# Strassen block products for layer 0's values, a ring of PSUM banks, and new hand-written orders in a two-layer attention kernel

## The chip, the cores and the metric

The kernel runs on one core of a Trainium2 chip. The metric is the device time of one launch in microseconds; lower is better. All large products are in float32. The engines are PE (TensorE matmul; its weight loads are listed as PEld), DVE (VectorE), ACT (ScalarE), POOL (GpSimd) and SP (SyncE, which here only issues DMAs).

## The reference, cut to what matters

```python
# layer 0: x is (8, 512, 32, 32): 8 batches, 512 channels, 1024 tokens
h = group_norm(x, 32 groups)                       # (8, 512, 1024)
q, k, v = einsum('oc,bcn->bon', qkv_w, h) + qkv_b  # 8 heads of 64
attn = softmax(q^T k / 8)                          # 1024 x 1024 per head
x = x + einsum('oc,bcn->bon', proj_w, attn v) + proj_b
# layer 1
importance = sum over channels of x*x;  idx = the 256 tokens of highest importance
q_sel, k_sel = layer_norm(wq x[idx]), layer_norm(wk x[idx]);  v = wv x
attended = softmax(clip(q_sel k_sel^T / sqrt(512))) v[idx]
x = x + wo (v with the columns idx replaced by attended)
```

## The kernel before

**Layer 0.** The unit of work is one pair of heads and one half (512) of the queries: 8 batches x 4 pairs x 2 halves = 64 units. In a unit, PE makes the scores of 8 blocks of 128 keys against 512 queries of two heads (`scores`), ACT copies them out of PSUM, DVE keeps the running maximum and subtracts it, ACT takes the exponential, POOL adds up the denominators (`add`), and PE multiplies with the values (`values`). Between these, PE does side work that other units need. `side(t)` lists up to seven pieces for unit t, and each has a `fill` (its matmuls) and an `empty` (one copy or add out of PSUM). They are

- q and k of a later pair, by `query_key`: Strassen's scheme with seven block products, four emptied by ACT and three by an add on DVE. It multiplies token sums (`combine_tokens`, made by POOL once per batch) with weight sums (`combine_weights`, made once at the start, stored in DRAM and loaded again tile by tile with `load_weights`, two ahead, on SP's queue);
- v for two pairs, a tile `vs[m]` of 1024 tokens x 256 columns, by `v_tokens`: four parts of two token blocks each, one per unit, all by plain products. A part is 16 calls of matmul with 64 token columns as weights and 256 columns streamed; float32 makes two instructions of each call;
- the output projection of the batch before, by `project_out`, in four of the eight units of a batch.

All side work goes through one PSUM bank (`ps_g`, one buffer); the chain of block products 1, 6, 7, 4 and that of 5, 3 stay in the bank from one fill to the next. The score tiles in SBUF, tagged "e", have 14 buffers (`ep`).

The order of everything in a unit is written out in the string `SLOT`: a word is a step, and each `+` or `-` says that it is done for a unit later or earlier. Each engine executes its instructions in this order.

**Layer 1** is ordered in the same way by the strings `BATCH` (one pass per batch) and `END` (the last two batches). The steps that are named later: `row` (four transposes of 128 tokens by PE) with `square` and `keep` (ACT) and `put` (DMA); `xs` (token sums by POOL); `va` to `vf` (PE: v by seven block products, `va` holds two of them) and `ka` to `kg` (ACT copies and DVE adds that take them); `count`, `place` and `pick` (DVE: rank of each token, and the 0/1 matrices that pick the highest 256); `holder` and `who` (indices of the picked tokens); `getx` and `getv` (gathers by POOL); `qk`, `stats`, `root`, `norm`, `normt`, `scale`, `score`, `clip`, `exp`, `probt`, `att`, `attk`, `attput` (the attention among the picked tokens); `fetch` (POOL puts the results in place), `back` (four transposes by PE) and `add` (DVE adds the residual and the result is stored). Every PE step of layer 1 writes one of eight PSUM banks, taken in `bank` from the pool "g" with eight buffers; which free bank is taken is left to the framework.

The tile for each v product of layer 0 is reached through these lines of `side`:

```python
m, part = divmod(t, 2 * NH)
...
if t and m + 1 < PAIRS // 2:
    todo[4] = v_tokens(m + 1, part)
```

Of the kernel before, what the change touches and what calls it, by code (L numbers as in the profile page):

```python
# [10 lines left out]
F32 = mybir.dt.float32  # L11
# [3 lines left out]
ALU = mybir.AluOpType  # L15
AX = mybir.AxisListType
PSUM = bass.MemoryType.PSUM
DRAM = bass.MemoryType.DRAM

P = 128  # L20
# [31 lines left out]
keep5+ val5- empty5- mix2- val4- sub1 sub6 fill0 empty0 den- take- mix1-- sc7+ out- exp6 var-  # L52
exp1 fac-- mean- sub0 sc6+ max6+ mix4- fill1 exp0 sub7 empty1 val6 max7+ val1 fill2 add1 add6
inv- app0- keep6+ exp7 keep7+ sub3 sub2 empty2 sc3+ app1- exp3 exp2 sc4+ fill3 mix3 max3+ stat1-
val7 empty3 add7 div- max4+ keep3+ keep4+ val0 fill4 add2 empty4 sc0++ turn+ neg+ sub5 sc1++
keep0++ add3 fill6 keep1++ val3 sub4 val2 exp5 add5 empty6 sc5++ max1++ sc2++ exp4 stat2+ add4
fill5 stat0 keep2++ spread0+ max5++ max2++
# [7 lines left out]
vput6- put4 keep2 back6--- row3 square3 square1 xs0 keep3 put3 keep1 put1 inv-- back7--- xs1 va1  # L65
back4--- row5 va0 add3--- ka0 add4--- att0-- vb0 kb0 ka1 row0 vput4- attk0-- row7 add6--- vd0
square0 holder- keep0 vc0 att1-- vb1 add7--- row6 who- kc0 put0 kg0 square7 kb1 kf1 keep7
square6 ve0 vd1 attk1-- va2 kd0 getx- vc1 square5 finite keep5 spread0 vput0- kc1 xs2 attput--
vput2- spread1 put2 vf1 ka2 vb2 kg1 kf0 vput3- imp0 imp1 fetch1-- count4 va3 count6 selt0-
selk0- fetch5-- selt1- fetch4-- ve1 vput7- selk1- keep6 count0 ka3 ke1 kf3 count1 kd1 qk1-  # L70
stats1- fetch0-- xs3 put5 qk0- count7 root1- fetch3-- qk2- norm1- kb2 put7 qk3- stats0- stats2-
root0- norm0- fetch2-- vd2 root2- kf2 back2-- stats3- fetch6-- norm2- kc2 fetch7-- vc3 vf0 vb3
root3- vput1- add2-- normt0- norm3- back5-- kb3 count2 vf2 back0-- ke0 vput5- ke2 normt1- add5--
normt2- vd3 scale2- vc2 normt3- scale0- add0-- scale3- kc3 put6 back1-- add1-- scale1- count3
kg3 score0- score1- row4+ square4+ keep4+ vf3 kg2 row1+ ve3 clip- kd3 ve2 kd2 count5 getv-
back3-- row2+ exp0- probt- ke3 square2+ place pick0 probk- pick1
"""
END = """
keep2- inv--- row5- row7- put4- put2- row0- row6- square1- keep1- att1--- holder-- square7-
who-- put1- attk1--- keep7- att0--- row3- put7- attk0--- square5- square6- square0- square3-  # L80
finite- va3- row0 attput--- keep5- keep3- back4---- getx-- xs2- spread0- add3---- vput0-- keep0-
xs3- add4---- back7---- back6---- fetch4--- put0- add7---- add6---- spread1- selt0-- imp0- imp1-
row7 selk0-- count3- selt1-- selk1-- qk0-- ka3- row4 put3- count6- qk1-- keep6- count0- square0
fetch0--- fetch5--- vput1-- stats0-- qk2-- keep0 root0-- row1 row6 count4- stats1-- norm0--
square7 put5- keep7 put6- put0 stats2-- root1-- count1- fetch3--- square1 root2-- square4 row5
va2- keep1 kf3- vput6-- square5 norm1-- ka2- put1 vput3-- keep4 vb3- qk3-- norm2-- fetch1---
count2- keep5 normt0-- put7 square6 kf2- fetch7--- row2 vput2-- count7- stats3-- kb3- vb2- put4
vc2- scale0-- keep6 row3 vd3- square3 kb2- vput7-- put6 va0- count5- square2 root3-- vd2- vc3-
kc2- finite fetch6--- keep3 kg2- vf2- ke2- keep2 spread0 fetch2--- place- norm3-- vput5-- ve2-
normt1-- vput4-- scale1-- kc3- spread1 kd2- xs0- va1- ka0- back2--- imp0 normt3-- pick1- pick0-  # L90
vput6- imp1 holder- kg3- scale3-- normt2-- vf3- scale2-- score1-- who- score0-- vb0- ka1- getx-
put5 ve3- kf0- count3 add2--- back6--- kb0- getv-- count5 clip-- vd0- kd3- vc0- selt0- put3 kc0-
xs1- add6--- count2 exp0-- back3--- kg0- vb1- probt-- selk0- selt1- vf0- count6 probk-- ke0-
selk1- put2 qk2- back7--- add3--- count1 ve0- kf1- ke3- count0 kb1- att1-- inv-- count7 attk1--
add7--- att0-- count4 back1--- place qk1- pick0 pick1 attk0-- kd0- qk0- holder who vd1- vc1-
back0--- kc1- getx stats0- stats1- attput-- fetch1-- fetch5-- root1- add0--- fetch4-- add1---
va2 vf1- root0- qk3- kg1- vput4- norm0- xs2 norm1- selt1 selt0 selk0 normt0- ve1- stats3- selk1
qk1 kd1- fetch2-- root3- fetch0-- stats1 normt1- ke1- norm3- vput7- scale1- stats2- back5--- qk3
qk2 root2- add5--- norm2- scale0- stats3 normt3- vput2- fetch3-- normt2- vput0- back0-- scale3-
scale2- vput1- vput3- root3 root1 back4--- qk0 score0- stats2 score1- vput5- ka2 kf2 norm1 root2  # L100
add0-- stats0 add4--- root0 back4-- xs3 norm3 va3 norm2 vb2 clip- vsel1 getv- fetch6-- norm0
back6-- add6-- exp0- normt2 normt3 kb2 ka3 normt1 add4-- vd2 probt- vb3 inv- probk- normt0
scale0 att0- scale2 att1- scale1 kb3 scale3 attk1- attk0- vc2 kc2 fetch7-- kg2 back5-- attput-
vf2 fetch7- ke2 score1 score0 fetch0- va0 vselk1 fetch2- ve2 back3-- ka0 clip exp0 back2-- vsel0
add5-- probt vd3 fetch6- inv vselk0 xs0 back1-- kc3 probk kf3 vc3 att0 add2-- add1-- att1 add3--
fetch3- fetch1- attk0 va1 attk1 kg3 back4- ve3 ka1 attput fetch5- back7-- kd2 kf1 fetch4- kd3
vb0 back6- kb0 kf0 vc0 add6- xs1 vb1 vd0 kb1 add7-- vd1 kc0 vf0 kc1 kg0 fetch6 ke0 vc1 ve0 kg1
ve1 fetch3 fetch2 add4- back3- fetch4 kd0 vf1 kd1 back2- fetch0 add3- add2- back5- ke1 vf3
back1- back0- fetch1 back7- add0- back0 add7- back4 back6 add5- add1- ke3 add0 fetch5 back2
fetch7 add4 add6 back7 back5 add2 add7 add5 back3 back1 add1 add3  # L110
# [3 lines left out]
def in_order(text):  # L114

    steps = []
    for word in text.split():
        name = word.rstrip("+-")
        ahead = word.count("+") - word.count("-")
        kind = name.rstrip("0123456789")  # L120
        steps.append((kind, ahead, int(name[len(kind):] or 0)))
    return steps


@with_exitstack
def attention_then_topk_attention(
# [103 lines left out]
    def bank(key):  # L230
        if key not in tiles:
            tiles[key] = pools["g"].tile(
                [P, C], F32, tag="g", name="b_" + "_".join(map(str, key))
            )
        return tiles[key]

# [19 lines left out]
    def keep_row(b, j):  # L256
        nc.scalar.copy(tiles["xT", b, j], tiles["pt", b, j])

# [19 lines left out]
    def imp(b, j):  # L278
        t = get("rp", ("imp", b), [P, N], "imp", 1)
        nc.scalar.copy(t[:, ts(j, HALF)], tiles["pi", b, j])  # L280

# [42 lines left out]

    def vkeep(b, j):
        nc.scalar.copy(values_of(b)[:, j, :], tiles["pv", b, j])

    SPAN = C // 2  # L330
# [1156 lines left out]
```

## Time and profile before

| what | value |
|---|---|
| median of 3 runs | 2411.2 us (2409.63 to 2411.27) |
| profiled execution | 2408.76 us, span of its instructions 2407.1 us |
| granted TensorE clock | 0.994 |
| busy share of the span | PE 98%, PEld 42%, DVE 80%, ACT 59%, POOL 60% |
| groups with most PE time | scores (L1133) 513.0 us, values (L1208) 488.4 us, q and k (L926) 231.0 + 169.8 us, v of layer 0 (L845, 128x256) 217.4 us, output projection (L845, 128x512) 208.2 us |

The durations come from the profiled execution. Its matmuls are pipelined: the mean of one matmul is its own latency, and the busy time of a group is the time in which at least one of it was in flight. "128*64 128x256" means weights of 128 rows and 64 columns, and an output of 128 partitions x 256 elements. Idle time stands before the instruction that ended it, with what released it.

### The profile page before, as it was taken

How to read it: one execution, taken by the hardware profiler on the slowest of the kernel's cores; microseconds unless marked ns; L12 is line 12 of the kernel's file. 1: busy time of each engine (PE TensorE's matmuls, PEld its weight loads, DVE VectorE, ACT ScalarE, POOL GpSimd, SP SyncE). 2: the span in 40 equal slices, each digit the busy share in tenths (PEclk: the TensorE clock that was granted, in tenths of full speed). 3: DMA queues.
4: the chain of work that ended last, by engine and by line, in shares of the span. 5: the costliest groups of instructions: out<-in, count | busy, mean ns of one | idle time of the engine just before them, and what ended most of it. 6: DMA issues, size and time to landing. Idle time of an engine off the chain costs nothing. (4 is left out here: it accounts for less than half of the span.)

```text
span 2407.1 us, 33474 instructions
## 1 busy us (share of the span) xinstructions
PE 2348.3 (98%) x11820; PEld 1012.5 (42%) x11820; DVE 1917.2 (80%) x3054; ACT 1429.8 (59%) x1948; POOL 1433.8 (60%) x885
## 2 busy tenths in 40 slices
PE   6999999999999999999999999999999989999998
PEld 2333333333333333333333333333333357777766
DVE  4989987897889779887988898788777467777885
ACT  2677766676577557756766676567666434333521
POOL 1568765875677567656766676577656434444343
PEclk9999999999999999999999999999999999999999
DMA  4122122212221222222212312212223434666654
GB/s 175 36 54 78 51 69 77 87 54 71 78 84 52 73 73 89 61 69 84 74 59 72 101 48 63 76 60 82 77 65 119 166 133 149 201 205 203 237 163 153
DMA packets 184391, 235.82 MB, mean 98 GB/s; under 512 B 40970, under 2 KB 94986, under 8 KB 184224
## 3 DMA queue, kind: packets, MB, share of 16 engines
q1 hardware_dynamic: 158560, 190.12, 24.5%
q10 hardware_dynamic: 18144, 31.48, 3.5%
q0 software_dynamic: 7520, 12.09, 1.9%
q8 instruction: 93, 1.52, 0.3%
q14 instruction: 74, 0.61, 0.1%
HBM read 174.08 MB, written 72.09 MB: 102 GB/s over the span
## 5 line engine op out<-in xcount | busy, mean ns | idle before, releaser
L1200 POOL TENSOR_TENSOR es<-es,e 128x1024 f32<-128x1024 f32 x384 | 918.5, 2392 | 133.0 <-ACT e L1195 112.8
L1141 ACT COPY e<-sc 128x1024 f32<-128x1024 f32 x512 | 508.1, 1013 | 241.0 <-PE sc L1133 158.2
L1192 DVE TENSOR_TENSOR e<-e,ns 128x1024 f32<-128x1024 f32 x512 | 600.2, 1205 | 6.4 <-ACT ns L1188 6.3
L1147 DVE TENSOR_TENSOR high<-sc,high 128x1024 f32<-128x1024 f32 x384 | 467.8, 1218 | 119.3 <-PE sc L1133 79.0
L1195 ACT ACTIVATE e<-e 128x1024 f32<-128x1024 f32 x512 | 520.5, 1060 | 26.1 <-DVE e L1192 18.3
L1133 PE MATMUL sc<-q,k 64*128 64x512 f32 x2048 | 513.0, 617 | 3.1 <-DVE high L1147 1.8
L1208 PE MATMUL av<-e,v 128*64 128x512 f32 x2048 | 488.4, 597 | 0.3 <-ACT e L1195 0.3
L1200 POOL TENSOR_TENSOR es<-e,e 128x1024 f32<-128x1024 f32 x64 | 152.5, 2383 | 487.6 <-PE g L926 316.9
L1133 PEld LDWEIGHTS sc<-q,k 64*128 64x128 f32 x2048 | 174.0, 185 | 285.6 <-issue 162.3
L1208 PEld LDWEIGHTS av<-e,v 128*64 128x64 f32 x2048 | 137.5, 136 | 310.1 <-issue 274.6
L926 PE MATMUL g<-wqkv,mix 128*64 128x512 f32 x960 | 231.0, 602 | 1.7 <-POOL wqkv L890 1.2
L845 PE MATMUL g<-wqkv,x 128*64 128x256 f32 x1920 | 217.4, 379 | 0.0
L845 PE MATMUL g<-o,wp 128*64 128x512 f32 x912 | 208.2, 598 | 0.0
L845 PEld LDWEIGHTS g<-wqkv,x 128*64 128x64 f32 x1920 | 137.8, 137 | 95.1 <-issue 27.8
L926 PE MATMUL g<-x,mix 128*64 128x512 f32 x720 | 169.8, 592 | 0.0
L977 DVE SCALAR_TENSOR_TENSOR xr<-g,pb,xr 128x512 f32<-128x512 f32 x56 | 42.1, 752 | 108.5 <-PE g L845 108.5
L926 PEld LDWEIGHTS g<-wqkv,mix 128*64 128x64 f32 x960 | 60.8, 136 | 156.0 <-issue 104.7
L385 ACT COPY V<-b_px 128x256 f32<-128x256 f32 x112 | 40.0, 376 | 141.5 <-PE b_px L371 104.7
L845 PEld LDWEIGHTS g<-o,wp 128*64 128x64 f32 x912 | 60.5, 136 | 140.7 <-issue 119.2
L472 PE MATMUL b_pp<-w,selT 128*128 128x512 f32 x256 | 112.3, 593 | 0.0
L1147 DVE TENSOR_TENSOR high<-sc,e 128x1024 f32<-128x1024 f32 x64 | 77.8, 1215 | 39.9 <-ACT e L1141 39.9
L964 ACT COPY v<-g 128x512 f32<-128x512 f32 x60 | 35.1, 585 | 123.2 <-PE g L845 123.1
(217 smaller groups left out, 2628.1 us busy)
## 6 DMA issues: line engine op xcount, KB each, us to landing
nb<-negd SPq DMA_DIRECT2D x128, 256.0 KB
x<-in_x_dram SPq DMA_DIRECT2D x32, 512.0 KB
ri<-rid SPq DMA_DIRECT2D x128, 128.0 KB
sx<-xT ACTq DMA_DIRECT2D x64, 256.0 KB
mix<-mixd SPq DMA_DIRECT2D x120, 128.0 KB
xr<-in_x_dram SPq DMA_DIRECT2D x58, 256.0 KB
x1d<-xr SPq DMA_DIRECT2D x58, 256.0 KB
sv<-V ACTq DMA_DIRECT2D x56, 256.0 KB
```

The costliest lines, as they stand in the source:

```text
L385: nc.scalar.copy(out_, bank(("px", b, i))[:, :SPAN])
L472: nc.tensor.matmul(pp, tiles["selT", b][:, k, ts(rb, P)], w["qk"[which]][:, k, :], start=(k == 0), stop=(k == CT - 1),)
L845: nc.tensor.matmul(out[r, :], wide_[:, r], moving, start=(k == 0), stop=(k == CT - 1),)
L926: nc.tensor.matmul(pt[r, :], weights[:, k, r], moving[:, k, :], start=(first and k == 0), stop=(k == 1), skip_group_check=True,)
L977: nc.vector.scalar_tensor_tensor(xr, po, pb[:, mt : mt + 1], xr, ALU.add, ALU.add,)
L1133: nc.tensor.matmul(sc[:, hh, :], ks[p][r, ts(j, P)], qs[p][r, ts(hf, HALF)], start=True, stop=True,)
L1141: nc.scalar.copy(raw[t, j], banks["s", t, j])
L1147: nc.vector.tensor_tensor(high[t], banks["s", t, j], raw[t, 0] if j == 1 else high[t], ALU.max)
L1192: nc.vector.tensor_tensor(raw[t, j], raw[t, j], high[t], ALU.add)
L1195: nc.scalar.activation(raw[t, j], raw[t, j], AF.Exp, scale=QK_SCALE)
L1200: nc.gpsimd.tensor_add(sums[t], raw[t, 0] if j == 1 else sums[t], raw[t, j])
L1208: nc.tensor.matmul(avs[t][HD * hh : HD * hh + HD, :], vs[p // 2][:, j, (p % 2) * P + HD * hh : (p % 2) * P + HD * hh + HD], e[:, hh, :], s ...
```

## The change

It has four parts.

1. v of the tiles m = 2 to 15 (all of batches 1 to 7) is made by `value_product0`: seven block products, with the token sums that q and k use already. A product is again 16 calls of matmul with 64 token columns as weights, but streams 128 columns. Four of the seven are copied out by ACT, three are added by DVE. The weight sums for v are made and stored by `combine_weights` beside those for q and k, and products 6, 7, 5 and 3 load theirs with `load_weights`; 1, 2 and 4 read `wqkv`. `v_tokens` stays for the tiles 0 and 1.
2. `products_of(t)` spreads the side work anew: of the eight units of a batch, the first gets four products of v, the second one, the third two, the seventh four, the eighth three. q and k stay where they were, and so does the output projection.
3. A class `Ring` hands out the eight banks of layer 1 and the 14 score tiles of layer 0: it gives the buffer that was given back first in the order of the program, by explicit `done` and `give` calls.
4. `SLOT`, `BATCH` and `END` are new orders of the same steps.

```diff
+class Ring:
+    def __init__(self, pool, tag, shape, n):
+        self.pool, self.tag, self.shape = pool, tag, shape
+        self.free, self.held = collections.deque(range(n)), {}
+    def take(self, key, name, uses=1):
+        i = self.free.popleft()
+        self.held[key] = [i, uses]
+        return self.pool.tile(self.shape, F32, tag=f"{self.tag}{i}", name=name, bufs=1)
+    def give(self, key):
+        if key in self.held:
+            self.held[key][1] -= 1
+            if not self.held[key][1]:
+                self.free.append(self.held.pop(key)[0])
...
+            pools["banks"] = Ring(ps, "bank", [P, C], 8)
...
+            scored = Ring(ep, "e", [P, 2, HALF], 14)
...
+            def products_of(t):
+                p, hf = divmod(t, NH)
+                b, at = divmod(t, NPAIR * NH)
+                plan = [None] * 7
+                if t and hf == 0 and p + 1 < PAIRS:
+                    plan[:3] = [("qk", p + 1, i) for i in ROUND[4:]]
+                elif hf == 1 and p + 2 < PAIRS:
+                    plan[:4] = [("qk", p + 2, i) for i in ROUND[:4]]
+                later = [n for n in FILLS if n > 2]
+                if at in (0, 6):
+                    m, places, which = 2 * b + 1 + at // 6, later, ROUND[:4]
+                elif at == 1:
+                    m, places, which = 2 * b + 1, [4], ROUND[4:5]
+                elif at == 2:
+                    m, places, which = 2 * b + 1, [3, 4], ROUND[5:]
+                elif at == 7:
+                    m, places, which = 2 * b + 2, [n for n in later if n > 3], ROUND[4:]
+                else:
+                    return plan
+                if 2 <= m < PAIRS // 2:
+                    for n, i in zip(places, which):
+                        plan[n] = ("v", m, i)
+                return plan
...
+            def value_product0(m, i):
...
+                def fill(pt):
+                    tokens = tokens_of(b, i)
+                    if i in MIXED:
+                        weights = mixed.pop(("v", m, i))
+                        load_weights()
+                    else:
+                        k, which = INPUT_WEIGHTS[i]
+                        weights = wqkv[:, 2 * k : 2 * k + 2, ts(2 * CT + 2 * hm + which, P)]
+                    for j in range(NB // 2):
+                        for k in range(2):
+                            for r in range(2):
+                                nc.tensor.matmul(
+                                    pt[ts(r, HD), ts(j, P)],
+                                    tokens[:, k, j * P + r * HD : j * P + r * HD + HD],
+                                    weights[:, k, :], start=(first and j + k == 0), stop=(k == 1),
+                                    skip_group_check=True,
+                                )
+                def empty(pt):
...
+                    if i in (1, 6, 7, 4):
+                        nc.scalar.copy(out, pv)
+                    else:
+                        nc.vector.tensor_tensor(out, pv, out, ALU.add)
```

The new `SLOT` takes PE's steps in this order: val5-, fill0, den-, sc7+, sc6+, fill1, val1, val0, fill2, sc3+, sc4+, fill3, val6, val2, fill4, sc0++, sc1++, val7, fill6, val3, sc5++, sc2++, fill5, val4. Before it was val5-, val4-, fill0, den-, sc7+, sc6+, fill1, val6, val1, fill2, sc3+, sc4+, fill3, val7, val0, fill4, sc0++, sc1++, fill6, val3, val2, sc5++, sc2++, fill5.

The end of `BATCH` and, where the next pass begins, its start; before:

```
... normt3- scale0- add0-- scale3- kc3 put6 back1-- add1-- scale1- count3 kg3 score0- score1- row4+
square4+ keep4+ vf3 kg2 row1+ ve3 clip- kd3 ve2 kd2 count5 getv- back3-- row2+ exp0- probt- ke3
square2+ place pick0 probk- pick1
vput6- put4 keep2 back6--- row3 square3 square1 xs0 keep3 put3 keep1 put1 inv-- back7--- xs1 va1
back4--- row5 va0 add3--- ka0 add4--- att0-- vb0 kb0 ka1 row0 vput4- attk0-- row7 add6--- ...
```

and after:

```
... normt3- kc3 vc3 kg2 scale2- scale3- back0-- score1- ke0 score0- row4+ add0-- put6 kg3 vf3 ve3
count3 square4+ clip- ve2 getv- kd3 keep4+ row1+ count5 place exp0- row2+ ke3 back3-- kd2 pick1
probt- square2+ pick0 probk-
row3 vput0- square3 put4 square1 inv-- xs0 va1 va0 keep3 back4--- put3 xs1 keep1 back7---
back6--- vput3- add3--- keep2 att0-- ka1 ka0 kf0 add4--- kf1 attk0-- row0 vb0 square0 kb0 keep0
att1-- put0 put1 vc0 add6--- vd0 kc0 holder- row6 row7 square7 add7--- row5 vb1 ...
```

## The prediction

> **What bounds the kernel now.** I read the page's totals first, then the busy times by stretch, then the groups by shape, then the timeline where the change acts.
>
> ```profile
> span 2407.1 us, 33474 instructions
> ...
> PE 2348.3 (98%) x11820; PEld 1012.5 (42%) x11820; DVE 1917.2 (80%) x3054; ACT 1429.8 (59%) x1948; POOL 1433.8 (60%) x885
> ```
>
> The stretches (us from the start; busy time and instructions of PE, PEld, DVE, ACT, POOL; granted clock, DMA share, GB/s) say where PE's idle 59 us lie:
>
> ```profile
> 240.00:1650.00 1410.00, 1410.00 (x7284) 506.82 (x7282) 1194.24 (x1560) 950.99 (x1133) 942.75 (x419) 1.00 0.23 70
> 516.00:540.80 24.80, 24.80 (x132) 8.98 (x130) 24.34 (x33) 18.41 (x22) 17.85 (x8) 1.00 0.16 49
> 540.80:574.00 33.20, 33.20 (x171) 12.04 (x170) 24.71 (x33) 20.16 (x25) 17.81 (x8) 1.00 0.23 72
> 638.10:669.30 31.20, 31.20 (x166) 11.18 (x165) 26.45 (x33) 18.38 (x21) 24.84 (x11) 1.00 0.22 74
> 2057.00:2118.40 61.40, 58.53 (x284) 43.79 (x284) 44.37 (x130) 23.55 (x59) 26.25 (x44) 0.97 0.63 213
> ```
>
> Row 1 is the middle of layer 0: PE has work in flight throughout. Rows 2 to 4 are three of a batch's eight units (one head pair, one half of the queries); all eight take 24.8, 33.2, 31.2, 32.9, 31.2, 26.0, 24.8 and 26.0 us, and PE is busy in all of each. So layer 0 lasts as long as PE streams, and a microsecond of matmul taken out there is one off the span, as long as DVE stays below PE. It is close in row 2 (24.34 of 24.80). Row 5 is one batch of layer 1: 2.9 us of PE idle, and clock 0.97.
>
> How fast PE streams is read from unbroken runs in the timeline (start, length, operation), for today's v and, later, for transposes:
>
> ```profile
> 705.20 0.20 PEld L1208 LDWEIGHTS av<-e,v 128*64 128x64 f32 x4 [0.76 <-issue]
> 705.68 0.14 PEld L1208 LDWEIGHTS av<-e,v 128*64 128x64 f32 x2 [0.28 <-issue]
> 706.54 0.14 PEld L845 LDWEIGHTS g<-wqkv,x 128*64 128x64 f32 x2 [0.29 <-DVE high L1147]
> 706.97 3.62 PE L845 MATMUL g<-wqkv,x 128*64 128x256 f32 x32
> 2234.94 1.78 PEld L247 LDWEIGHTS b_pt<-ident,x 128*128 128x128 f32 x16
> 2235.04 1.91 PE L247 MATMUL b_pt<-ident,x 128*128 128x128 f32 x16
> ```
>
> A v part is 32 instructions, 16 pairs: two 64-column halves of the array work side by side. Less the last one's 0.38, 3.62 us are 15 steps of 0.216: 256 columns a pair. The transposes stream 128 columns, each with a load of its own: (1.91 - 0.27)/15 = 0.109 us. Half the columns take half the time.
>
> **Part 1: v by seven products.** Two v tiles per batch, batches 1 to 7: 14 tiles. Before, a tile is 4 parts x 16 pairs x 0.216 = 13.8 us. After, it is 7 products x 16 pairs, each streaming 128 columns: at 0.109 that is 12.2. Saved 1.6 us a tile, 14 x 1.6 = 22.2 us, all on the path.
>
> The trace shows no 64-wide pair at 128 columns, so its spacing is the unknown. Below: 0.107, half of 0.216 without the fixed part. Above: 0.141, if each matmul waits for its own load to end (a pair of loads shows 0.14). I take 0.109. The transposes' single loads last as long (1.78 us for 16 is 15 x 0.109 + 0.14) and yet keep 0.109, so the matmul does not wait for a load's shown end; and four loads in 0.20 us, where two take 0.14, mean that a second pair starts 0.06 after the first. Loading occupies a half for about 0.06 of 0.109.
>
> A rule speaks against this: the Trainium skill, "TensorE: Matmul & The Clock Gate", section "Back-to-back issue gap", gives streams of load and matmul about 81 ns at 128 columns against 56 ns for a matmul alone. Those 25 ns on each pair would make an estimated 0.134 x 112 = 15.0 us a tile, and the change 17 us slower in layer 0; the transposes above, at 0.109 with a load each, do not show such a surcharge.
>
> The new products need no further change of array form: each sits beside an av group, 128*64 too, and the first loads of g (706.54) go out while av still runs.
>
> **Part 2: what rides along.** ACT keeps 4 copies of 128x512 per tile (0.585 each): nothing. DVE gets 3 adds per tile, 42 x 0.69 (the q and k adds at L945) = 29 us, beside PE. Per unit, PE loses a part (3.45) and gains 4, 1, 2, 0, 0, 0, 4, 3 products of 1.745: 28.3, 31.5, 31.2, 29.5, 27.7, 22.6, 28.3, 27.8 us. DVE's fullest unit becomes the fifth, 26.45 of 27.7 (95%), where it was the first (98%); the third and eighth, with two and three adds, reach 26.3 of 31.2 and 25.2 of 27.8. So PE stays the bound. If that cover went, the adds would cost up to 29 us.
>
> 56 more weight loads of 128 KB go through SP, behind the stores and reloads of the maxima and sums, which wait for DVE and ACT. They go out two fills ahead, as q and k's do now, for which PE never idles: nothing; uncovered, the nearest row is a 0.8 us weight-load wait on a DMA, 14 x 0.8 = 11 us. At the start POOL makes four more sums, half the size of L900's 2.34 us, 4.7 us together, and SP four more stores behind them. POOL's first adds are some 60 us in, and it is busy for 10.8 of the first 60 us: nothing; uncovered, 5 us.
>
> **Part 3: layer 1, ring and orders.** The same matmuls, so only waits can change.
>
> ```profile
> PE b_pt L247 <- DVE y L625: 8.5, 3, 2.8
> ```
> ```profile
> 2113.43 1.89 PE L371 MATMUL b_px<-w,x 128*128 128x256 f32 x8
> 2114.20 3.64 DVE L407 TENSOR_SCALAR pick<-iota_f,place 128x256 bf16<-128x256 f32 x8
> ...
> 2115.16 0.60 PE L617 MATMUL b_po<-ident,V 128*128 128x128 f32 x4
> ...
> 2117.84 1.26 DVE L625 TENSOR_TENSOR y<-b_po,y 128x512 f32<-128x512 f32 x2
> 2118.56 1.12 PE L247 MATMUL b_pt<-ident,x 128*128 128x128 f32 x4 [2.80 <-DVE y L625]
> ```
>
> Three times a row transpose waits 2.8 us for its PSUM bank, which add frees; add stands on DVE behind eight picks. The granted clock then drops for a while: 0.97 over 61.4 us is 1.8 us. Together 4.6, three times: 13.9 us.
>
> What decides is the time from the last score matmul to that transpose. PE before: nine groups of four transposes (0.44), three value products (4 x 0.216 = 0.86) and one va (1.73) make 8.3 us. DVE before: clip, takes, count5, place, pick and the first add take from 2107.3 to 2118.5, 11.2 us. 11.2 - 8.3 = 2.9, which is the wait. In the new order row5 has moved back. Following take and done through it, the first row that gets an add's bank is row0, which gets add3's; it comes after nine transpose groups, the three products, two va (3.5) and att0 (1.7): 11.7 us. DVE has the same steps ahead of add3, and count3, now before clip, with add0 and kg3 takes 3.1 of the 3.45 us of the scores. So 11.2 against 11.7: the wait should go, with only 0.5 us in hand; next come the banks of add4, add6 and add7, each with two or more us in hand. I keep 1 us a boundary: 11 us saved. Bounds: 13.9 saved, and below nothing as much lost if another bank is late.
>
> The last two batches (END) are reordered too. PE idles 14 us from 2180 on; some 9 of these are waits in END that an order can gain, and as much could be lost: I take nothing.
>
> **Sum.** The profiled execution: 2408.8 us, span 2407.1. 2408.8 - 22.2 - 11 = 2375.6. It lies 2.4 under the median of 2411.2, so the forecast is 2378.
>
> **Rivals.** (a) *The weight loads set the pace.* At 0.141 a pair, a tile takes 15.8 us; against the forecast 14 x 112 x 0.032 = 50 us, so 2428, slower. It decides from 0.130 a pair, where layer 0's loss eats layer 1's 11 us. For it: no such pair is in the trace. Against it: transposes and load spacing. (b) *Ring and orders give layer 1 nothing*: the bank still waits for an add, or another wait takes its place. For it: 0.5 us in hand. Then 2389. (c) *The side bank is handed over late.* All side work shares one bank, and 50 instead of 44 fills per batch pass through it; a product's 1.7 us is half a part's. With 0.3 us exposed on each of 98 products, 29 us: 2407. Against it: two units of each batch hand over seven times already, with no idle PE.
>
> **How the numbers follow.** Forecast 0.72, (a) 0.07, (b) 0.13, (c) 0.08. Low end: 22.2, 13.9 and 9 all gained, 2366; I put 2365. High end: (b) with 9 us lost in END and a few on (c)'s way: 2402. The rest of (c) and (a) lie beyond. About 0.2% (5 us) is what a measurement of this kernel tells from no change. Faster: the forecast, (b), and a little of (c): 0.87; within: 0.03; slower: (a) and the rest of (c): 0.10.
>
> **What would show it.** v's matmuls: 16 pairs in about 1.9 us. Units of 28.3, 31.5, 31.2, 29.5, 27.7, 22.6, 28.3, 27.8 us, PE busy in all of each; layer 0 some 22 us shorter. No PE wait on add in layer 1 and no lowered clock between batches. A v group of 2.3 us or more, or PE idle before g in layer 0, would prove me wrong.

## The result, and the profile after

The kernel after takes 2419.4 us (median of 7 runs, 2413.3 to 2421.4) against 2411.3 us before: 1.0030 times the time, 95% interval 1.0019 to 1.0041. A second set of 10 runs gave 2414.2 us, ratio 1.0022 (1.0011 to 1.0032). The forecast was 2378 us. The change makes the kernel slower by 5 to 8 us instead of faster by 33.

The profiled execution of after took 2421.0 us, its span 2419.1. From the page's totals:

```profile
span 2419.1 us, 36720 instructions
...
PE 2332.1 (96%) x13164; PEld 1055.1 (44%) x13164; DVE 1970.2 (81%) x3096; ACT 1423.0 (59%) x1948; POOL 1437.9 (59%) x889
```

PE's busy time did fall, by 16 us, while the span grew by 12. So the work was saved, and PE idled 28 us more. The busy times by stretch say where. The columns are as in the prediction; the rows are the middle of layer 0, then the first, second, fourth, fifth and sixth unit of one batch:

```profile
240.00:1650.00 1410.00, 1388.85 (x8476) 545.16 (x8474) 1233.27 (x1589) 936.04 (x1123) 933.89 (x416) 1.00 0.24 75
```
```profile
526.10:554.30 28.20, 28.20 (x232) 13.95 (x230) 25.71 (x32) 19.72 (x25) 17.81 (x8) 1.00 0.18 53
554.30:585.80 31.50, 31.50 (x174) 11.55 (x173) 23.29 (x32) 19.58 (x24) 17.79 (x8) 1.00 0.25 76
617.00:646.70 29.70, 29.70 (x142) 9.29 (x140) 28.02 (x41) 19.86 (x24) 18.30 (x8) 1.00 0.27 82
646.70:675.10 28.40, 28.22 (x130) 8.67 (x128) 27.07 (x33) 17.77 (x20) 23.08 (x10) 1.00 0.25 80
675.10:701.20 26.10, 23.26 (x106) 6.88 (x104) 21.13 (x27) 19.04 (x24) 22.42 (x11) 1.00 0.41 133
```

In the middle of layer 0, PE was in flight for all of 1410 us before; now it idles 21 us. The first, second and fourth unit last what was predicted (28.3, 31.5, 29.5), and PE fills them. The fifth and the sixth were predicted at 27.7 and 22.6; over batches 1 to 6 they average 29.3 and 25.5. In the fifth, DVE is busy for 27 to 29 us; in the sixth nothing is near full, so a chain of waits sets the length. The eight units then sum to 231.3 us a batch; before they took 230.0, and 226.9 were predicted. For comparison, the fourth and the sixth unit of a batch before:

```profile
605.20:638.10 32.90, 32.90 (x172) 11.75 (x170) 26.08 (x41) 20.52 (x25) 18.69 (x8) 1.00 0.23 72
669.30:695.30 26.00, 26.00 (x139) 9.41 (x137) 20.96 (x27) 20.26 (x25) 18.34 (x10) 1.00 0.39 134
```

What PE waits for most in that stretch of after (us, times, longest); before had no entry there:

```profile
PE sc L1265 <- DVE high L1279: 10.3, 9, 1.9
PE den L1359 <- ACT e L1273: 6.1, 4, 1.8
```

The price of a product was right. In the timeline (start, length), 16 pairs of 128 columns take 1.92 us, (1.92 - 0.27)/15 = 0.110 a pair, where 0.109 was assumed:

```profile
539.34 1.92 PE L1064 MATMUL g<-mix_v,wqkv 128*64 128x128 f32 x32
```

**A DVE operation that became up to 3.5 times as long.** L805 before and L851 after are the same instruction, the group norm's apply; each row gives its shortest, median and longest ns.

```profile
L805 DVE TENSOR_SCALAR x<-x,gsc,gsh x30: 760/799/814, 24.3 to 1568.3; 128x1024 f32<-128x1024 f32 x30
```
```profile
L851 DVE TENSOR_SCALAR x<-x,gsc,gsh x30: 803/1732/2859, 24.9 to 1587.4; 128x1024 f32<-128x1024 f32 x30
```

The timeline of DVE and POOL in a fourth unit of after shows why:

```profile
861.64 1.27 POOL L1395 TENSOR_TENSOR o<-o,ri 128x512 f32<-128x512 f32 x1
861.93 0.69 DVE L1291 TENSOR_REDUCE quarter<-mT 128x16 f32<-128x512 f32 x1
862.53 3.69 DVE L851 TENSOR_SCALAR x<-x,gsc,gsh 128x1024 f32<-128x1024 f32 x2
862.86 2.81 POOL L1332 TENSOR_TENSOR es<-es,e 128x1024 f32<-128x1024 f32 x1
866.15 0.83 DVE L1303 STREAM_TRANSPOSE four<-quarter 32x32 f32<-32x32 f32 x4
```

The two applies stand next to each other now (`app1- app0-`), between the maxima's `turn` and `neg`. POOL's add ends at 865.67, and the second apply at 866.22: it sat behind the add and then needed 0.55 us. All 24 applies of this trace that took over 0.85 us began while POOL was in an operation and ended 0.55 us after it. The old order had other DVE work between the two; in the same batch before they took 0.76 and 0.81 us:

```profile
842.21 0.76 DVE L805 TENSOR_SCALAR x<-x,gsc,gsh 128x1024 f32<-128x1024 f32 x1
842.46 5.73 POOL L1200 TENSOR_TENSOR es<-es,e 128x1024 f32<-128x1024 f32 x2
842.88 2.35 DVE L1192 TENSOR_TENSOR e<-e,ns 128x1024 f32<-128x1024 f32 x2
845.15 0.81 DVE L805 TENSOR_SCALAR x<-x,gsc,gsh 128x1024 f32<-128x1024 f32 x1
```

These lay beside POOL's adds too, but each began within the last 0.22 us of one, and the next add gave way: the two here take 2.74 and 2.91 us where 2.38 is usual. So it matters at what point of an add the apply comes. Now the applies cost the fourth unit 3.8 us of DVE instead of 1.6, the fifth 3.4, and every `neg` behind them comes later. In the fourth unit PE still fills the time. The length of the fifth goes with theirs: over batches 1 to 6 they take 2.6 us in two units of 28.4, 3.7 in three of 29.5, and 4.4 in one of 30.3 (in the second execution 2.6, 3.7 and 4.2 in units of 28.4, 29.5 and 31.7).

The Trainium skill, "SBUF — State Buffer", section "Who interferes with whom", says why such an instruction can block: DVE in a 2-port mode, which `tensor_scalar` may enter, contends with GpSimd for a shared port pair, and whoever issues first keeps it for its whole instruction. It says too that a DVE instruction with two inputs in SBUF contends with a GpSimd instruction that reads SBUF. The rows agree: 2.85 us where 0.76 to 0.81 is usual, with an end 0.55 us after the add's; the ports themselves are not in the trace.

**The same at the start.** POOL's weight sums run beside the first batch's group norm (timeline, DVE and POOL):

```profile
15.08 2.34 POOL L958 TENSOR_TENSOR mix<-wqkv 128x1024 f32<-128x1024 f32 x1 [12.90 <-DMA wqkv<-in_qkv_wT_dram]
15.14 2.31 DVE L190 TENSOR_TENSOR rs_t_gn<-rs_y_gn 128x4 f32<-128x4 f32 x1
17.48 0.16 DVE L191 TENSOR_TENSOR rs_t_gn<-rs_t_gn,rs_ve 128x4 f32<-128x4 f32 x1
...
24.85 6.73 DVE L851 TENSOR_SCALAR x<-x,gsc,gsh 128x1024 f32<-128x1024 f32 x4
```

An operation on 128x4 takes 2.31 us, as long as the sum beside it, and 0.16 when alone. Four did so before as well; the four new sums of v now lie beside the applies, 6.73 us for four that took 3.0. The first scores start at 41.0 us instead of 38.7. This varies: in the second execution (e9) the sums met the group norm at another point, the four applies took 10.05 us, and the scores started at 37.9.

**The sixth unit.** SP's issues in the timeline, and then ACT's copy of the maxima:

```profile
685.29 3.02 SPq L754 DMA_DIRECT2D x<-in_x_dram  x4
690.75 0.33 SPq L1309 DMA_DIRECT2D negd<-neg  x1
695.36 0.81 SPq L1314 DMA_DIRECT2D nb<-negd  x2
698.48 0.59 ACT L1320 COPY ns<-nb 128x512 f32<-128x512 f32 x1 [1.88 <-DMA nb<-negd]
```

The x of the batch after next, 2 MB, is issued ahead of the 4 KB of maxima; these need 4.6 us until their reload can be issued, and ACT waits. The same loads were there before, but in a unit that PE filled for 26.0 us. Batch 6 has no further x to load and no statistics of it to make. There the sixth unit lasts 22.9 us in the same execution, near the predicted 22.6, and PE fills it; in batches 1 to 5 it lasts 25.8 to 26.3:

```profile
1601.80:1624.70 22.90, 22.89 (x107) 6.96 (x107) 19.74 (x24) 19.07 (x24) 19.98 (x10) 1.00 0.20 59
```

**Layer 1**, from its first row transpose to the end: before, after, and a second profiled execution of after (e9).

```profile
1934.10:2407.10 473.00, 443.24 (x2136) 324.32 (x2136) 338.33 (x971) 170.89 (x430) 198.39 (x323) 0.98 0.53 179
```
```profile
1948.00:2419.10 471.10, 437.74 (x2136) 323.36 (x2136) 335.80 (x971) 170.75 (x430) 198.33 (x323) 0.98 0.54 179
```
```profile
1951.90:2408.80 456.90, 433.85 (x2136) 321.47 (x2136) 336.29 (x971) 170.69 (x430) 198.62 (x323) 0.99 0.55 184
```

The row transposes no longer wait for `add`, in either. In the first execution other waits had taken most of the gain. One is new: `vd3` waits for the DVE step `kf3`, which the new `BATCH` has put behind `norm3`, `add5`, `add2` and `add1`. In layer 1 of that execution PE's waits begin with

```profile
PE b_px L399 <- DVE V L417: 15.8, 4, 9.2
PE b_px L399 <- DVE y L665: 3.9, 2, 2.0
```

and in the second it is 6.8 us for the first of these and none for the second. The 9.2 us is one wait, of the first product with a token sum in layer 1, which took 5.4 us before and 7.0 in the second. `vd3` waits four times, 9.6 us together in the first (twice with `add` as the last to come, which is the second row) and 6.0 in the second. So the same program's layer 1 varies by 14 us.

### The profile page after: what moved, and what is told of

Its sections match the earlier page's. It is cut to its first block, busy times and chain, and to the rows that moved or that the text cites. A ratio compares the mean times of both kernels' runs of the same rounds, so it can differ in the third digit from the quotient of the medians.

```text
span 2419.1 us, 36720 instructions
## 1 busy us (share of the span) xinstructions
PE 2332.1 (96%) x13164; PEld 1055.1 (44%) x13164; DVE 1970.2 (81%) x3096; ACT 1423.0 (59%) x1948; POOL 1437.9 (59%) x889
## 3 DMA queue, kind: packets, MB, share of 16 engines
q1 hardware_dynamic: 175392, 198.51, 25.8%
## 4 chain that ended last, share of the span: by engine, by line
PE 78%; DVE 14%; DMA 4%; issue 2%; ACT 1%; POOL 0%; another core or an unknown queue 0%; SPq 0%; DVEq 0%; ACTq 0%; POOLq 0%
PE sc L1265 16%; PE av L1343 14%; PE g L1024 13%; PE g L891 9%; PE g L1064 7%; PE b_px L399 4%; DVE high L1279 3%; PE b_pp L507 3%; DVE e L1324 2%; PE b_py L399 2%; DMA nb<-negd 1%; PE den L1359 1%; PE first L891 1%; DMA negd<-neg 1%; PE b_pa L622 1%
## 5 line engine op out<-in xcount | busy, mean ns | idle before, releaser
L1327 ACT ACTIVATE e<-e 128x1024 f32<-128x1024 f32 x512 | 531.3, 1061 | 218.2 <-DVE e L1324 212.2
L1324 DVE TENSOR_TENSOR e<-e,ns 128x1024 f32<-128x1024 f32 x512 | 608.7, 1204 | 19.3 <-ACT ns L1320 18.0
L1273 ACT COPY e<-sc 128x1024 f32<-128x1024 f32 x512 | 501.8, 1016 | 109.1 <-PE sc L1265 71.4
L1343 PE MATMUL av<-e,v 128*64 128x512 f32 x2048 | 500.0, 599 | 1.1 <-ACT e L1327 0.6
L1343 PEld LDWEIGHTS av<-e,v 128*64 128x64 f32 x2048 | 135.7, 137 | 276.3 <-issue 231.3
L1024 PE MATMUL g<-wqkv,mix_qk 128*64 128x512 f32 x960 | 230.9, 602 | 1.3 <-POOL wqkv L936 1.3
L1024 PE MATMUL g<-x,mix_qk 128*64 128x512 f32 x720 | 169.8, 592 | 0.0
L1024 PEld LDWEIGHTS g<-wqkv,mix_qk 128*64 128x64 f32 x960 | 60.9, 136 | 155.3 <-issue 118.0
L1395 POOL TENSOR_TENSOR o<-o,ri 128x512 f32<-128x512 f32 x64 | 82.1, 1282 | 32.3 <-DMA ri<-rid 31.3
L1279 DVE TENSOR_TENSOR high<-sc,e 128x1024 f32<-128x1024 f32 x64 | 77.0, 1204 | 25.7 <-ACT e L1273 25.7
L1024 PEld LDWEIGHTS g<-x,mix_qk 128*64 128x64 f32 x720 | 51.8, 137 | 103.5 <-issue 88.3
L1290 DVE STREAM_TRANSPOSE mT<-high 128x512 f32<-128x512 f32 x128 | 90.4, 706 | 2.0
```

Source lines behind the costliest of these rows:

```text
L1024: nc.tensor.matmul(pt[r, :], weights[:, k, r], moving[:, k, :], start=(first and k == 0), stop=(k == 1), skip_group_check=True,)
L1273: nc.scalar.copy(raw[t, j], banks["s", t, j])
L1279: nc.vector.tensor_tensor(high[t], banks["s", t, j], raw[t, 0] if j == 1 else high[t], ALU.max)
L1324: nc.vector.tensor_tensor(raw[t, j], raw[t, j], high[t], ALU.add)
L1327: nc.scalar.activation(raw[t, j], raw[t, j], AF.Exp, scale=QK_SCALE)
L1343: nc.tensor.matmul(avs[t][HD * hh : HD * hh + HD, :], vs[p // 2][:, j, (p % 2) * P + HD * hh : (p % 2) * P + HD * hh + HD], e[:, hh, :], s ...
```

## The experiments

Theory 1: PE's saving is real, but the units that it was taken from (fifth, sixth, and those of batch 0) are bound by DVE, which stands behind POOL, and by the maxima's way through DRAM; in layer 1 one wait was exchanged for another. Rivals: the new unit order itself costs (rival 2); the new orders of layer 1 cost (rival 4); DVE or the queue doesn't matter. Ratios are to before, run on the same chip.

| run | median us | ratio, 95% interval |
|---|---|---|
| e1 old SLOT | 2447.9 | 1.0147 (1.0130 to 1.0164) |
| e2 plain v | 2456.6 | 1.0193 (1.0172 to 1.0214) |
| e3 old BATCH, END | 2419.2 | 1.0043 (1.0028 to 1.0057) |
| e4 x after neg | 2455.8 | 1.0184 (1.0167 to 1.0201) |
| e5 apply on ACT | 2397.7 | 0.9951 (0.9933 to 0.9968) |
| e6 applies apart | 2433.3 | 1.0100 (1.0083 to 1.0117) |
| e7 sums wait | 2403.9 | 0.9980 (0.9970 to 0.9990) |
| e8 x after take | 2408.2 | 0.9990 (0.9978 to 1.0002) |
| e9 after again | 2414.2 | 1.0022 (1.0011 to 1.0032) |
| e10 = e5 + e8 | 2398.4 | 0.9955 (0.9940 to 0.9970) |
| e11 rings only | 2398.3 | 0.9958 (0.9941 to 0.9975) |
| e12 = e10 + e7 | 2387.8 | 0.9920 (0.9901 to 0.9938) |
| e13 e5, x in four | 2392.2 | 0.9935 (0.9914 to 0.9956) |
| e14 e13, sums wait, kf3 | 2375.2 | 0.9857 (0.9841 to 0.9873) |
| e15 e14, first batch | 2372.2 | 0.9847 (0.9831 to 0.9864) |
| e16 e11, sums wait | 2395.7 | 0.9938 (0.9919 to 0.9958) |

### Parts undone

**e1**: `SLOT` of before.

> The kernel after with the unit order (SLOT) of before; v by seven products, ring, BATCH and END stay. Theory 1 (light units are bound by something else than PE): the light units (fifth, sixth) and the loaded ones are the same whatever the order, and the new order only softens it; the result stays at the time after or above, 2415 to 2430 us. Rival 2 (the new order itself costs, the products are fine): layer 0 gains its 22 us, some 2397 us.

2447.9 us: even above the expected span. PE's waits in the middle of layer 0 are now 24.5 us for `sc <- DVE high` and 14.5 us for `sc <- ACT e`. The new order is worth 28 to 30 us to the seven products; rival 2 falls. The applies take 0.76 to 0.81 us again after the start, yet the fifth unit lasts 30.0 us: in the old order other waits bind it.

**e2**: plain v, new order.

```diff
-                later = [n for n in FILLS if n > 2]
-                ...
+                if t > 1 and t // 4 + 1 < PAIRS // 2:
+                    todo[4] = v_tokens(t // 4 + 1, t % 4)
```

> The kernel after with v by the four plain parts in the units where they stood before, without v's weight sums at the start; new SLOT, ring, BATCH and END stay. Theory 1: the new order costs nothing by itself, layer 0 is as long as before the change, and the start's 2 us come back: layer 0 12 to 15 us shorter than after, 2404 to 2408 us in all. Rival 2 (the order costs): PE gets 22 us of work more under the same slow order, 2420 to 2440 us.

2456.6 us, outside both ranges. Its waits in the middle of layer 0:

```profile
PE g L891 <- DVE x L851: 33.0, 6, 5.5
```

The fifth unit grows to 38.9 us on average: its v part needs all of the normalised x, and the new order puts the applies late. So this run is no price of the order; order and spread only work together.

**e3**: `BATCH` and `END` of before, on the ring.

> The kernel after with BATCH and END of before on the new ring of banks; layer 0 is untouched. Theory 1: in layer 1 the new order only exchanged the waits of the row transposes on add for the waits of vd3 on kf3; with the old orders the row waits come back, the time is 0 to 4 us longer than after, 2419 to 2423 us. Rival 4 (the new orders cost): 2408 us. What was predicted (the new orders save 11 us): 2430 us.

2419.2 us, the time that theory 1 gave, but not for its reason: the trace has no row transpose waiting for `add`, though the order is the old one, and layer 1 takes 462.7 us. That asks for the ring by itself:

**e11**: plain v and all three orders of before; only the two rings are left.

> The kernel after with plain v, and SLOT, BATCH and END of before: only the ring of banks in layer 1 and the ring of score tiles in layer 0 are left of the change. Theory 1: the ring alone, which frees a bank in the order of its last use, ends the row transposes' wait on add (with the old orders on the ring these waits were absent), so layer 1 takes 460 to 463 us instead of 473 and the time is 2397 to 2402 us. Rival (the new orders bring it): layer 1 472 us, 2409 to 2412 us.

2398.3 us, 9.9 below before. Layer 1:

```profile
1935.70:2395.50 459.80, 438.71 (x2136) 320.94 (x2136) 337.83 (x971) 171.55 (x430) 198.31 (x323) 0.99 0.54 183
```

It is 13 us shorter than before, and the row transposes' waits on `add` are gone. Layer 0's units are as before. So the ring carries most of layer 1's gain. With the old orders on the ring, layer 1 took 460, 463 and 468 us in three profiles (e11, e3, e16); with the new ones 457 to 462 in eleven of twelve. That leaves a few us at most for the new orders. And after lies 16 us above e11 (2414.2, measured beside it): that is what v's products and the new orders cost together.

**e9**: after, unchanged.

> The kernel after, unchanged, once more. Layer 1 (from its first row transpose to the end) took 471 us in the profile after, but 457 to 460 us in six experiments with the same layer 1. If layer 1 varies from run to run, this profile shows 457 to 460 us and a time of some 2408; if it is a matter of this program, 470 us and 2419 us.

Layer 1 took 456.9 us here, and the profiled execution 2410.8 us; the median of 10 runs is 2414.2. Layer 1's 471 us were that execution's. Layer 0 was slower in turn: from the first to the last unit's denominator 1819.6 us against 1812.5.

### What DVE waits for

**e5**: apply on ACT in batches 1 to 7.

```diff
-                if b == 1 and c % 2:
+                if b >= 1:
```

> The kernel after with the group norm's apply (x, L851, two per fourth and fifth unit) done by ACT for batches 1 to 7 instead of DVE. In the trace after, one of the two takes 2.85 us and lies wholly inside an es add of POOL (2.8 us); before, each took 0.76 to 0.81. Theory 1 (DVE full in the light units, because x stands behind POOL): DVE loses 3.8 and 3.4 us in the fourth and fifth unit, the fifth falls from 29.3 to its PE time 27.7, the sixth, whose maxima start earlier, falls too by up to 1 us: 9 to 15 us less, 2404 to 2410 us. Rival (the way of the maxima through DRAM binds these units, DVE doesn't): within 3 us of after, 2416 to 2421 us.

2397.7 us, more than expected. Fourth, fifth and sixth unit:

```profile
612.60:642.20 29.60, 29.60 (x142) 9.41 (x143) 24.72 (x39) 21.87 (x26) 17.81 (x8) 1.00 0.25 81
642.20:670.30 28.10, 27.97 (x133) 8.74 (x131) 25.07 (x31) 19.82 (x22) 23.14 (x11) 1.00 0.25 81
670.30:696.10 25.80, 23.22 (x106) 6.87 (x104) 21.07 (x27) 19.04 (x24) 21.00 (x10) 1.00 0.41 134
```

DVE has fallen from 28.0 to 24.7 us in the fourth unit, and the fifth, 28.1, is within 0.4 us of what PE needs. Against after the ratio falls by 0.007 to 0.008, 17 to 19 us: the largest gain of a single edit here. The profiles put less of it into layer 0, which is 10 us shorter than in one profile of after and 17 than in the other; 7 to 9 of these are the fifth units. The edit takes the whole apply off DVE, also the 1.6 us per unit that it takes undisturbed, so it is no exact price of the blocking. The sixth stays.

**e6**: the applies moved on DVE.

```diff
-... inv- sub3 exp6 sc3+ empty2 exp7 max3+ ... turn+ app1- app0- neg+
+... inv- app0- sub3 exp6 sc3+ empty2 app1- exp7 max3+ ... turn+ neg+
```

> The kernel after with only the place of the two applies moved, still on DVE: app0 right behind inv, app1 behind empty2, ahead of the maxima's turn as in the old order, not adjacent and not between turn and neg. Theory 1: x takes 0.8 to 1.6 us instead of 1.9 and 1.7 on average, and neg comes 2 to 4 us earlier in the fourth and fifth unit: 5 to 10 us less, 2409 to 2414 us. Rival (DVE time doesn't matter there): 2416 to 2421 us.

2433.3 us: a miss. The median apply fell only from 1.73 to 1.53 us, and now `sub3` and `max3` stand behind it on DVE. ACT's exponential waits for the one (1.6 us in one fifth unit) and its copy of a score bank for the other (1.8 us), and PE waits for that copy:

```profile
663.85 2.55 PE L1265 MATMUL sc<-q,k 64*128 64x512 f32 x6 [2.41 <-ACT e L1273]
```

The fifth unit takes 31.8 us. So the applies were not free of POOL's adds in this place either, and what stands behind them there is waited for at once. Other places were not tried.

**e7**: the weight sums at the start wait for the first batch's normalised x.

```diff
+                    if not n:
+                        nc.gpsimd.tensor_copy(s[0][:, 0, :1], hs[0][:, CT - 1, :1])
```

> The kernel after with POOL's eight weight sums at the start made to wait (by a copy of one column of the last normalised x) until the first batch is normalised. In the trace after, four vector operations of 128x4 take 2.3 us instead of 0.16 and the four applies 1.72 to 1.75 us instead of 0.8, each side by side with a sum on POOL. Theory 1 (DVE stands behind POOL): 4 x 2.15 + 4 x 0.95 = 12.4 us of the start go, first scores at some 29 us instead of 41, 2405 to 2409 us. Rival (the start is set by the weights' arrival and PE): 2416 to 2421 us; at most the 2.3 us that the start has lost against before.

2403.9 us. The timeline of DVE:

```profile
15.52 0.16 DVE L835 SCALAR_TENSOR_TENSOR gsc<-rs_y_gn,gw 128x4 f32<-128x4 f32 x1
15.72 0.16 DVE L837 TENSOR_TENSOR gsh<-gm,gsc 128x4 f32<-128x4 f32 x1
15.91 0.16 DVE L838 TENSOR_TENSOR gsh<-gb,gsh 128x4 f32<-128x4 f32 x1
16.11 2.98 DVE L851 TENSOR_SCALAR x<-x,gsc,gsh 128x1024 f32<-128x1024 f32 x4
```

Every operation is back to its own length. The first scores come at 31.1 us instead of 41.0. Most of these 9.9 us were lost before as well: the first scores came at 38.7 to 39.9 us in three profiles without v's weight sums, and at 37.9 to 41.0 in ten with them.

### The sixth unit and the x load

**e4**: x issued behind `neg` instead of at `div`.

> The kernel after with one thing moved: the loads of the next x (4 x 512 KB, once per batch, sixth unit) are issued after the maxima's store and reload of that unit instead of just ahead of them. Theory 1 in its narrow form (the maxima's way through DRAM, queued behind 2 MB, ends the sixth unit): the sixth unit falls from 25.4 to some 23 us in six batches, 12 to 16 us less, 2403 to 2407 us. Rival (DVE alone binds that unit, or the chain is as long without the load): no change, 2417 to 2421 us.

2455.8 us: the opposite. DVE's statistics read x in the same unit and now wait for it, and all of DVE with them:

```profile
DVE bs L801 <- DMA x<-in_x_dram: 45.8, 7, 6.9
```

**e8**: x issued behind `take`, earlier in the unit.

> The kernel after with the loads of the next x (2 MB, sixth unit) issued earlier in the same unit, right after the denominators' take, so that neither the statistics that read x nor the maxima's store and reload stand behind them. Theory 1, second half (the sixth unit is bound by the maxima's way through DRAM behind the 2 MB): the sixth unit falls from 25.4 to some 23 us, 10 to 15 us less, 2404 to 2410 us. Rival (the queue doesn't matter, DVE of the unit before binds): 2416 to 2421 us.

2408.2 us, 8 to 10 below after by the ratios, as theory 1 has it. By the traces less is sure: the sixth unit averages 24.6 us instead of 25.5, and layer 0 is as long as in one profile of after and 8 us shorter than in the other.

**e10**: e5 and e8 together.

> Both edits to the light units: the group norm's apply on ACT (batches 1 to 7) and the loads of the next x right behind take. With the apply on ACT alone the sixth unit still took 25.1 us. Theory 1 (what is left there is the maxima's way through DRAM, behind 2 MB): the sixth unit falls to 22.6 to 23.2 us, and the time by 10 to 14 us below the apply on ACT alone, 2384 to 2389 us. Rival (the two edits hide the same wait): 2395 to 2399 us.

2398.4 us: the time is the rival's, nothing is added to e5, and the sixth unit averages 25.7 us. PE's waits in the middle of layer 0 name the new one:

```profile
PE g L1024 <- DMA mix_qk<-in_qkv_wT_dram: 10.9, 5, 2.7
```

Now the weight loads stand behind the 2 MB. Behind `neg`, ahead of `neg` or behind `take`: each place makes somebody wait. **e12** (with e7's edit) agrees:

> Apply on ACT, x behind take, and the weight sums of the start made to wait, together. If the three causes add up: 2397.7 (apply on ACT) less 10 to 14 (x) less 9 to 12 (start) gives 2372 to 2379 us, some 1.4% below before. If they hide one another: 2385 to 2395 us.

2387.8 us, some 10 below e10: the start's share adds, the x load's does not.

**e13**: e5, and the 2 MB as four loads in four units.

```diff
+                        if name == "out" and t > CT:
+                            b, c = divmod(t - CT - 1, NPAIR * NH)
+                            if c < CT and b + 2 < B:
+                                load_x(b + 2, [c])
```

> Apply on ACT, and the 2 MB of the next x in four loads of 512 KB, one behind take in each of the sixth, seventh, eighth and next first unit, each in the unit whose statistics read it. Theory 1 (a block of 2 MB on SP's queue ends the sixth unit, by the maxima when it is ahead of neg, by the weight loads when it is ahead of those): the sixth unit falls to 22.6 to 23.2 us, 13 to 16 us in six batches, 2382 to 2386 us. Rival (the maxima's chain needs 25 us by itself): 2395 to 2399 us.

2392.2 us: by the ratios 4 us less than e5, not 13 to 16, with intervals that overlap; layer 0 is 10 us shorter in the profiles. SP's issues in the same unit, and the unit:

```profile
683.14 0.34 SPq L1312 DMA_DIRECT2D negd<-neg  x1
684.50 0.81 SPq L1317 DMA_DIRECT2D nb<-negd  x2
```
```profile
667.20:691.80 24.60, 23.16 (x110) 6.87 (x110) 21.55 (x28) 19.23 (x24) 19.32 (x10) 1.00 0.24 77
```

From the maxima's store to their reload it is now 1.36 us where it was 4.61, as theory 1 has it, but the unit averages 24.1, not 22.6 to 23.2. The block was 1 us of it; in what remains PE waits up to 1.4 us for `sc <- DVE high`, with DVE not full (21.6 of 24.6). Here too batch 6, without load and statistics, needs 22.9 us, the others 24.3 to 24.6. So the rest comes with the 512 KB that are still loaded there or with the statistics, 1.5 us of DVE; which of the two stays open.

### What it is worth without the waits

**e14**: e13, e7 and `kf3` moved from behind `add1` to behind `kb3` in `BATCH`.

> e13 with the weight sums of the start made to wait and with kf3 moved up in BATCH, from behind add1 to behind kb3. Theory 1: 9 us less at the start, and four waits of vd3 on kf3, 1.6 us each, go (6 us): 2366 to 2372 us. If the row transposes or another step wait instead of vd3: 2373 to 2377 us. If e13 brings nothing: 2382 to 2388 us.

2375.2 us, in the range of the second case but not for its reason: layer 1 takes 454 us, has no wait of `vd3` on DVE, and beside it only two small waits that e9 lacks (1.5 and 1.0 us); what is missing is what e13 was short of. The two added edits were not run one by one.

**e15**: e14, with v's third tile by plain parts in batch 0.

> e14 with the first batch's share undone: v's third tile (for the first two pairs of batch 1) by four plain parts in the fifth to eighth unit of batch 0, where DVE and not PE sets the length. Theory 1: these four units fall from some 106 to 102 us, 3 to 5 us less than e14. Rival (the units of the first batch are as long whatever PE does): PE's 1.6 us more, 0 to 3 us above e14.

2372.2 us: 3 us less, the expected time, but hardly by the expected way. The four units fall only from 104.6 to 103.7 us in the profiles, and 2 us of the difference lie in layer 1 (453.9 against 451.8), which the edit doesn't touch. From its page:

```profile
span 2369.7 us, 36509 instructions
...
PE 2321.8 (98%) x13068; PEld 1047.8 (44%) x13068; DVE 1917.0 (81%) x3067; ACT 1450.3 (61%) x1974; POOL 1431.2 (60%) x890
```

It beats both kernels: 1.5% below before, 42 to 47 us below after. PE is back at 98%.

**e16**: e11 with e7's edit.

> Plain v and all orders of before, with the two rings, and with the weight sums of the start made to wait. If DVE stood behind POOL at the start of before as well (four operations of 2.3 us in its trace): 8 to 9 us below the rings alone, 2388 to 2391 us. Against e14 and e15 it tells what seven products are worth when the waits are gone: by theory 1 they are some 16 to 22 us faster than this.

2395.7 us (2388.3 to 2399.1), 5 above the expectation: the first scores come at 30.9 us instead of 39.9, so the start's 9 us are there, but layer 1 took 468 us in the profiled execution. Against e15, layer 0 is 8 us longer (1800.2 against 1792.1 us between the first and the last unit's denominator). e15 has the apply on ACT and x in four loads besides; in e16's units PE is in flight throughout (1410.00 of 1410 us in the middle of layer 0), so these would gain it little (that was not run). So with these waits gone the seven products and their order are worth some 8 us in layer 0, less than half of the 21 that PE saves.

## Why the prediction was wrong

- **Part 1, the price of a product: right.** 0.110 us a pair against 0.109 (bounds 0.107 to 0.141); neither rival (a)'s 0.141 nor the estimated 0.134 shows. Six of eight units have the predicted length to 0.2 us. At 0.110 the products save PE 21 us, a little under the 22.2 that were reckoned (where "14 x 1.6" is 22.4).
- **Part 1, "all on the path": wrong.** The step that failed is "So PE stays the bound". It compared PE's new time with DVE's old busy time, operation by operation as long as before, and took PE's sum as the length of every unit. In the fifth unit the reordered `SLOT` put the applies inside POOL's adds; the unit took 29.3 us instead of 27.7, some 10 us over six batches, and e5 gets 28.1 with the applies off DVE. The new order was costed at nothing as a whole; its moved steps were not looked at one by one, and POOL was read only as an engine with time to spare, not as one that DVE can stand behind.
- **The sixth unit** is the larger miss, some 17 us over six batches. 22.6 us was PE's sum alone, and it came true only in batch 6, which loads no x (22.9). In the others a chain through DRAM behind a 2 MB load, and DVE's statistics of that x, stand in a unit that had 26.0 us of PE to hide them before. e13 shows 1 us of the 2.9 to be the block of loads; the rest is not settled.
- **The first batch.** It has no output projection, and PE is not all that binds there. Its fifth to eighth units took 102.1 us before and 106.5 after, though PE lost some 1.5 us of work in them. Without its part of v the fifth takes 24.6 us in e14 and with it 26.6 in e15: 3.45 us of PE are worth 2.0 there. e15 got 1 us back in these units.
- **Part 2.** DVE's adds cost nothing that shows in the units that got them, and PE never waits for v's weights there. "POOL makes four more sums: nothing; uncovered, 5 us" came close: by the ten profiles with these sums against the three without it is about 1 us, not by lateness of POOL's adds but by DVE standing behind the sums. POOL's first add comes 78 us in, not 60.
- **Part 3: the size was about right, its carrier wrong.** The row transposes' waits on `add` are gone, and layer 1 gains 5 to 13 us by the ring alone (e11, e3, e16; one profile of before). The new order, from which the 11.7 against 11.2 us were reckoned, was not needed for that, and brought a wait of its own (`vd3` on `kf3`), the "other wait" of rival (b). In the first profile layer 1 gained only 2 us, 9 less than forecast; in the second 16.
- **The rivals.** None named a DVE operation that gets longer. (c) came near in time (2407), by another mechanism: no side bank was late. The slower rival (a) was the wrong mechanism.

## What to carry to other kernels

Work taken out of one engine counts only in stages where that engine binds by more than is taken out; ask of each lightened stage what was hidden under it, including chains of small DMAs behind large loads. When an order is rewritten, look at each moved DVE operation for what POOL runs when it starts: its length is not its own. A batch that lacks a step, like batch 6 without the load, is an experiment that the trace already holds. And a change with several parts is best measured one by one: here the unnoticed ring was the gain, and the main idea paid only after several waits were taken from it.

## What the runs showed of the hardware

A 128x4 operation on DVE took 2.31 us instead of 0.16 beside a sum on POOL, a 128x1024 apply up to 2.86 instead of 0.8. The apply ended 0.55 us after the POOL operation that was running when it began. Where the apply began just before an add, the add took 2.7 to 2.9 us instead of 2.4. The scores' shift (L1324), of the same size, with its second input in PSUM, keeps its 1.2 us beside the same adds. A 4 KB store issued 2.4 us after a 2 MB load's last issue took 4.6 us until its reload could be issued, 1.4 where no such load was near. And the same 2136 matmuls of layer 1 took 457 to 471 us in different executions of one program.
